# Both sequences of a pair in one low-rank product and one update

## The chip, the cores and the metric

The kernel runs on one core of a Trainium2 chip, all in float32. The metric is the device time of one execution in microseconds; of several executions the median is given. Beside it stands one execution that the hardware profiler recorded, with its own time and its span, from the first to the last instruction of the program.

## What is computed

Two layers with a residual each, on x of 8 sequences, 256 tokens, 1024 features:

```
# layer 0: one of several lora_A per sequence, rank 32
x = x + (x @ W0.T + (x @ lora_A0[i0[b]]) @ lora_B0.T * 0.5)
# layer 1: one of 32 adapters per sequence, rank 16, and a bias
x = x + (x @ W1.T + b + (x @ lora_A1[i1[b]]) @ lora_B1[i1[b]] * 2)
```

## The kernel before

**One matrix for both layers.** Both layers are linear, so the kernel multiplies them once: M = (W0 + 1)^T (W1 + 1)^T, of 1024 x 1024, and the output is x M plus an update of low rank for each sequence. This preparation takes the first 124 us of the span. After it come the 8 sequences in four pairs (the loop at L1164, `q` = 0 to 3).

**Seven products instead of eight, twice.** A pair's x has 256 tokens of each of two sequences, and 1024 features. It is cut into four blocks: `x["11"]` and `x["12"]` are the two halves of the features of the pair's first sequence, `x["21"]` and `x["22"]` those of the second. M is cut in four as well, and Winograd's form of Strassen's algorithm needs seven products of blocks, of sums of blocks (`Pair.sums_1` to `sums_4`) and of sums of M's blocks (`ops`). Each of the seven is done in the same way once more, on quarters: `product` (L517) runs seven steps of two matmuls each, 128x128 by 128x256, for which VectorE makes four sums of x's quarters (`z_sums`, L477) and `Operand.sums`, `sums_rest` those of M's (for the first pair these are made within the loop, under `early`). The fourth sum is an operand called `t4`.

**PSUM.** The eight banks are two sets of four, X and Y. A product fills the seven quarters of one set (`slot`, `BANK`); the next product goes to the other set. In Winograd's form some products add up on one another: with `first` False a product is accumulated on what its set holds. After a product the set is copied out by ScalarE (`keep`, L506) or added by VectorE to what was kept (`add_up`, L510: four additions, the bank of step 6 first and that of steps 3 and 4 last); `form` (L574) turns seven quarters into a block of 256 by 512, and `store` writes it out. In one turn of the loop, with P1 to P7 for its seven products:

| product | set | x operand | VectorE or ScalarE after it |
| --- | --- | --- | --- |
| P1 | X | x11 | keep(kept1) |
| P2 | Y | s1 | keep(kept5) |
| P3 | X, added to P1 | s2 | keep(kept2) |
| P4 | Y, added to P2 | s4 | add_up(kept2), form, store: first sequence, right half |
| P5 | X, added to P3 | s3 | add_up(kept5), form, store: second sequence, right half |
| P6 | Y, new | x12 | add_up(kept1), form, store: first sequence, left half |
| P7 | X, added to P5 | x22 | form from kept2 and X in the next turn: second sequence, left half |

In the table s1 to s4 stand for the sums in the code's order (`sq(0)` to `sq(3)`). X and Y change places from pair to pair.

**The low-rank part before.** For a sequence `b`, `down` (128 x 8 chunks x 64 columns) holds the down projections: 32 columns of layer 0 and 16 of layer 1 (the latter already multiplied with W0). `low_start` (L776) is one product with M = 64 output rows: TensorE's columns 0 to 63 take the first half of the features, columns 64 to 127 the second half at the same time, in 8 matmuls, and ScalarE scales the result and sets a row of ones for the bias (L788). The two partial sums must be added: `low_end` (L796) multiplies with the matrix `join`, which adds them, adds the cross term of the two layers, and writes the sum twice, into rows 0 to 63 and rows 64 to 127; ScalarE copies it back (L806). There is one such pair of calls for each sequence: for the pair's first sequence in P7 of the pair before (for the first pair in the last product of the preparation, the call of `chain.product` at L1136), for its second sequence in P1.

**The updates before.** `update` is low (256 tokens x 64 rows) times `up` (64 rows x 1024 columns: layer 0's up projection, layer 1's, and the bias). `add_update` (L536) adds it onto the accumulators of a product, in the slots 3, 2, 4 and 5: four matmuls that contract over 64 rows. They alternate between rows 0 to 63 and 64 to 127, which both hold the same sequence, so that two may run side by side in TensorE's rows. The stationary side is the low product of one half of the tokens, or the difference of both (`diff`, VectorE, L851); the moving side is a quarter of `up`'s columns, or for P7 the difference of `up`'s left and right half (`up21`, VectorE, L863). There is one update in P4 (first sequence, right half), P5 (second, right), P6 (first, left) and P7 (second, `up21`), after the product's third step.

**The order of the work** is written out by hand (`manual_schedule`): each engine's queue has the program's order, and semaphores are set between engines. TensorE, ScalarE, VectorE and GpSimd each run one queue; SP issues the loads, GpSimd most stores. In the preparation's last product ScalarE's queue has L788, L806, then the copy L1146; VectorE's queue has there `form(chain.keep5, X, ...)` at L1147, whose first instruction (L591) reads what L1146 copied, and behind it, in order, the sums for the first pair's M operands, `z_sums`, `pair.sums_2` (L841) and the first turn of the loop. `up` and `join` have two tiles each, one per sequence of a pair; `down` too.

Of the kernel before, what the change touches and what calls it, by code (L numbers as in the profile page):

```python
# [20 lines left out]
P = 128  # L21
# [3 lines left out]
MLOW = 64  # L25
ONES = 112
BIAS = 48
# [15 lines left out]
def kernel(  # L43
# [66 lines left out]

    joins = [const.tile([P, 2, MLOW], F32, tag=f"join{i}", name=f"join{i}") for i in range(NU)]
    cross = const.tile([P, B, R1], F32, tag="cross", name="cross")
    downs = [const.tile([P, NK, MLOW], F32, tag=f"down{i}", name=f"down{i}") for i in range(NV)]
    lows = a1.rearrange("p (n k) b r -> p n (k b r)", n=NLOW)
    diffs = [const.tile([P, P], F32, tag=f"diff{i}", name=f"diff{i}") for i in range(2)]
    s_all = const.tile([P, 2 * 4 * NB * P], F32, tag="s_all", name="s_all")
# [95 lines left out]

    def load_up(b: int):
        i = index(fixed1, b, N1)
        for copy in range(2):
            nc.sync.dma_start(
                ups[b % NU][copy * MLOW + R0 : copy * MLOW + RR, :],
                lora_b1[bass.ds(i, 1)].rearrange("o r d -> (o r) d"),
            )
# [294 lines left out]
    def low_region(ps):  # L514
        return ps[3][:, NQ:NH]

    def product(ps, x, z, op, first, update=None, low=None, plan=None, apart=None):  # L517

# [17 lines left out]
        def add_update():  # L536
            rows, diff, c0, c1 = update
            t0, t1 = rows[:, 0:P], rows[:, P:T]

            for n, (i, stat, mov) in enumerate(  # L540
                ((3, diff, c1), (2, t0, c0), (4, t1, c0), (5, t1, c1))
            ):
                half = slice(n % 2 * MLOW, (n % 2 + 1) * MLOW)
                into(i, stat[half], mov[half], False)

# [9 lines left out]
        if plan is None:  # L555
            plan = [1, 2, 4, add_update if update else None, 6, 5, 7, 3]
            if low:
                plan[5:5], plan[8:8] = low[:1], low[1:]
        for step in plan:
            if step == 0:  # L560
                add_update()
            elif callable(step):
                step()
            elif step is not None:
                a, b = operands[step]
                if step == 3 and apart is not None:
                    started.discard(BANK[3][0])
                for c in range(2):
                    into(step, a[:, c, :], f[b][:, c, :], c == 1, apart if step == 3 else None)

    def home(i: int):
        return work[:, i * NV7 * NQ : (i + 1) * NV7 * NQ]
# [202 lines left out]

    def low_start(b: int, x_b, pl):  # L776
        down = downs[b % NV]
        for k in range(NB):
            for half in range(2):
                nc.tensor.matmul(  # L780
                    pl[half * MLOW : (half + 1) * MLOW, :],
                    down[:, half * NB + k, :],
                    x_b[half][:, k, :],
                    start=(k == 0),
                    stop=(k == NB - 1),
                    skip_group_check=True,
                )
        nc.scalar.activation(  # L788
            lows[:, b % NLOW],
            pl,  # L790
            mybir.ActivationFunctionType.Identity,
            bias=shift[:, 0:1],
            scale=scale[:, 0:1],
        )

    def low_end(b: int, pl):  # L796
        low = lows[:, b % NLOW]
        nc.tensor.matmul(  # L798
            pl,
            joins[b % NU].rearrange("p u r -> p (u r)"),  # L800
            low,
            start=True,
            stop=True,
            skip_group_check=True,
        )
        nc.scalar.copy(low, pl)  # L806

    def fill_join(b: int):
        for half in range(2):
            rows = slice(half * MLOW, half * MLOW + R0)  # L810
            for copy in range(2):
                nc.gpsimd.tensor_scalar_mul(
                    joins[b % NU][rows, copy, R0:RR], cross[rows, b, :], L1_SCALING
                )

# [3 lines left out]
    class Pair:  # L819
# [4 lines left out]
        def __init__(self, q: int):  # L824
            self.q, self.b = q, (2 * q, 2 * q + 1)
            self.x = {}
            self.first, self.second = (sets[q % 2], sets[(q + 1) % 2])
            self.low = [lows[:, b % NLOW] for b in self.b]
            self.z = [z_homes[(NV7 * q + i - 1) % 3] for i in range(NV7)]
# [18 lines left out]

        def diff(self, n: int):
            low = self.low[n]  # L850
            nc.vector.tensor_tensor(diffs[n], low[:, 0:P], low[:, P:T], ALU.subtract)  # L851

        def update(self, n: int, h: int):
            cols = [ups[n][:, h * NH + i * NQ : h * NH + (i + 1) * NQ] for i in range(2)]
            return (self.low[n], diffs[n], *cols)

        def update21(self):

            return (self.low[1], diffs[1], up21[:, 0], up21[:, 1])

        def up21_sum(self):
            up = ups[1].rearrange("p (h i n) -> p h i n", h=2, i=2)
            nc.vector.tensor_tensor(up21, up[:, 0], up[:, 1], ALU.subtract)  # L863

    def end(pair, X, Y, v, w):
# [26 lines left out]
        def o22():  # L892
# [3 lines left out]
        plan = (  # L896
            0,
            lambda: nc.scalar.copy(v3, slot(X, 3)),
# [13 lines left out]
        )  # L912
        product(
            X, pair.xq("22"), pair.z[6], ops["t4"], False, pair.update21(), plan=plan, apart=p3
        )
        add(at(v, 3), p3, v3)
# [10 lines left out]
    with tc.manual_schedule(engines=ORDERED):  # L927
# [34 lines left out]
        nc.gpsimd.memset(shift, 0.0)  # L962
        nc.gpsimd.memset(shift[96:P], 1.0)
        nc.gpsimd.memset(shift[96:ONES], 0.0)
        nc.gpsimd.memset(fold, 0.0)
# [5 lines left out]
        for i in range(NV):  # L971
            nc.gpsimd.memset(downs[i], 0.0)
        for i in range(NU):
            nc.gpsimd.memset(joins[i], 0.0)
            for copy in range(2):
                sides = [ident[:, u * MLOW : u * MLOW + RR] for u in range(2)]
                nc.gpsimd.tensor_tensor(joins[i][:, copy, 0:RR], sides[0], sides[1], ALU.add)
                nc.gpsimd.tensor_copy(
                    joins[i][:, copy, BIAS : BIAS + 1], ident[:, ONES : ONES + 1]
                )  # L980

# [81 lines left out]
        for i in range(NU):  # L1063
            for copy in range(2):
                row = copy * MLOW + BIAS
                nc.sync.dma_start(ups[i][row : row + 1, :], bias1.rearrange("(o d) -> o d", o=1))
        for b in range(2):
            load_up(b)
        for i, which in enumerate(("21", "22")):
# [11 lines left out]
        for b in range(2):  # L1081
            fill_down(b)
            fill_join(b)
        one.product7()
# [38 lines left out]
        for which in ("21", "22"):  # L1123
# [17 lines left out]
            low=(  # L1141
                lambda: low_start(0, (pair.x["11"], pair.x["12"]), low_pl),
                lambda: low_end(0, low_pl),
# [15 lines left out]
        def load_down_later(b):  # L1159
            load_down(b)  # L1160
            fill_down(b)
            fill_join(b)

        for q in range(B // 2):  # L1164
            more = q + 1 < B // 2
            xs = pair.x
            early = q == 0
# [18 lines left out]
            if more:  # L1186
                load_next("11", "12", "21")
                load_down_later(after[0])
            kept1, kept5, kept2 = home(q % 2), home((q + 1) % 2), home(2)


            for task in pending:
                task()
            pl = low_region(Y)
            product(
                X,
                pair.xq("11"),
                pair.z[0],
                ops["11"],
                True,  # L1200
                low=(
                    lambda: low_start(b1_, (xs["21"], xs["22"]), pl),
                    lambda: low_end(b1_, pl),
                ),
            )
            keep(kept1, X)
            z_sums(pair.sq(1), pair.z[2])
            pair.diff(0)
            if early:
# [9 lines left out]
            if early:  # L1219
                ops["22"].sums_rest()  # L1220
                ops["21"].sums_dma()
            pair.diff(1)
            z_sums(pair.sq(3), pair.z[3])
# [15 lines left out]

            product(Y, pair.sq(3), pair.z[3], ops["22"], False, pair.update(0, 1))  # L1240
            if early:
# [6 lines left out]

            product(X, pair.sq(2), pair.z[4], ops["t3"], False, pair.update(1, 1))
            form(kept2)  # L1250
# [9 lines left out]

            product(Y, pair.xq("12"), pair.z[5], ops["21"], True, pair.update(0, 0))
            if more:
# [4 lines left out]
            if not more:  # L1267
# [12 lines left out]
                False,  # L1280
                pair.update21(),
                low=(
                    lambda: low_start(after[0], (following.x["11"], following.x["12"]), pl7),
                    lambda: low_end(after[0], pl7),
                ),
# [6 lines left out]
            following.sums_4()  # L1292
            for b in after:
                load_up(b)

# [47 lines left out]
```

## Time and profile before

| | us |
| --- | --- |
| median of 3 runs | 336.69 (335.87 to 337.17) |
| profiled execution | 336.44 |
| its span | 334.7 |
| TensorE busy | 329.2 |
| VectorE busy | 258.6 |
| ScalarE, GpSimd busy | 64.4, 65.3 |

The span is cut into 40 slices of 8.4 us, with a digit for the busy share of each engine in tenths. The granted clock of TensorE is 1.00 over the whole span. A line of the timeline gives the start, the length, the engine, the code's line, what is written and read, and the shape. `128*128 128x256` is a matmul with 128 rows and 128 columns of the array in use and a moving side of 256 columns; `64*128` uses half of the rows, `128*64` half of the columns. A matmul of the program makes two rows in float32. The length of a matmul is that of its way through the array; how close two follow is read from their starts. L526 is the line of `product`'s matmuls, L780 that of `low_start`, L798 that of `low_end`, L512 that of `add_up`, L486 that of `z_sums`, L436 that of `sums_rest`.

### The profile page before, as it was taken

What the parts mean: (1) busy time and instruction counts of PE and PEld (TensorE: products, weight loads), DVE (VectorE), ACT (ScalarE), POOL (GpSimd) and SP (SyncE); (2) the same over time, 40 slices, a digit from 0 to 9 for tenths busy, and PEclk for the clock granted to TensorE, in tenths of its full rate; (3) what the DMA queues carried; (4) which work ended last, traced back from release to release, by engine and by line L of the source; (5) the groups of instructions that cost most, each with busy time, mean ns of one, the idle gap of its engine ahead of it and who ended that gap; (6) DMA issues with size and microseconds to landing.
All of it is one profiled execution on the core that took longest, in us unless ns stands there. A gap on an engine that the chain in (4) does not pass through costs nothing.

```text
span 334.7 us, 4532 instructions
## 1 busy us (share of the span) xinstructions
PE 329.2 (98%) x1520; PEld 249.1 (74%) x1520; DVE 258.6 (77%) x498; ACT 64.4 (19%) x138; POOL 65.3 (20%) x121
## 2 busy tenths in 40 slices
PE   8999999999999999999999999999999999999996
PEld 8888434544488877888877887877888777788875
DVE  5886799569899999999997856985675986323964
ACT  1042224300034132440001330001330001322000
POOL 7003021540042232772023100012200010000000
DMA  7929992990062980686267400286400121100113
GB/s 213 208 94 192 227 241 58 161 178 21 2 94 66 197 132 14 110 135 105 95 179 210 85 0 0 77 217 158 111 8 0 65 94 63 66 0 1 65 63 125
DMA packets 66400, 34.53 MB, mean 103 GB/s; under 512 B 47301, under 2 KB 61125, under 8 KB 66377
## 3 DMA queue, kind: packets, MB, share of 16 engines
q1 hardware_dynamic: 56520, 21.13, 28.0%
q0 software_dynamic: 7680, 12.59, 17.6%
q10 hardware_dynamic: 2176, 0.52, 0.9%
q8 instruction: 12, 0.20, 0.2%
q14 instruction: 12, 0.09, 0.1%
HBM read 19.55 MB, written 8.39 MB: 83 GB/s over the span
## 4 chain that ended last, share of the span: by engine, by line
PE 87%; DMA 5%; DVE 3%; SPq 2%; ACTq 1%; issue 1%; ACT 0%; DVEq 0%
PE bank L526 66%; PE bank L285 10%; PE bank L780 4%; DMA units<-in_L_cond_W_dram 4%; PE bank L734 2%; DVE w1T L224 2%; PE bank L990 2%; SPq L170 2%; DMA work<-in_L_cond_lora_As_dram 1%; PE bank L798 1%; SPq L178 1%; ACTq L197 0%; DVE w1T L232 0%; ACTq L140 0%; PE bank L712 0%
## 5 line engine op out<-in xcount | busy, mean ns | idle before, releaser
L512 DVE TENSOR_TENSOR work<-bank,work 128x512 f32<-128x512 f32 (+1 forms) x56 | 32.7, 619 | 19.0 <-PE bank L526 18.8
L508 ACT COPY work<-bank 128x512 f32<-128x512 f32 (+1 forms) x60 | 27.6, 546 | 45.5 <-PE bank L526 45.0
L921 POOL DMA_DIRECT2D out_dram<-work x12 | 9.0, 754 | 101.4 <-DVE work L597 101.4
L526 PE MATMUL bank<-w0n,w1T 128*128 128x256 f32 x104 | 24.6, 384 | 0.0
L788 ACT ACTIVATE a<-bank,shift,scale 128x256 f32<-128x256 f32 x8 | 4.5, 564 | 103.3 <-PE bank L780 103.3
L224 DVE STREAM_TRANSPOSE w1T<-units 128x512 f32<-128x512 f32 (+1 forms) x20 | 17.5, 912 | 6.4 <-DMA units<-in_L_cond_W_dram 6.3
L526 PEld LDWEIGHTS bank<-w0n,w1T 128*128 128x128 f32 x104 | 19.3, 190 | 4.1 <-issue 1.7
L526 PE MATMUL bank<-w1T,s_all 128*128 128x256 f32 x88 | 22.3, 379 | 0.0
L526 PE MATMUL bank<-w0n,m 128*128 128x256 f32 x88 | 21.2, 384 | 0.0
L237 DVE STREAM_TRANSPOSE units<-units 128x512 f32<-128x512 f32 x32 | 19.9, 678 | 0.2
L526 PEld LDWEIGHTS bank<-w0n,m 128*128 128x128 f32 x88 | 16.4, 190 | 3.4 <-issue 1.4
L526 PEld LDWEIGHTS bank<-w1T,s_all 128*128 128x128 f32 x88 | 16.7, 190 | 2.3
L526 PE MATMUL bank<-tw,m 128*128 128x256 f32 x68 | 17.5, 382 | 0.0
L526 PE MATMUL bank<-tw,s_all 128*128 128x256 f32 x64 | 16.1, 379 | 0.0
L780 PE MATMUL bank<-units,down 128*64 128x256 f32 x128 | 15.6, 385 | 0.0
L526 PE MATMUL bank<-m,units 128*128 128x256 f32 x64 | 15.1, 379 | 0.0
L990 PE MATMUL bank<-w1T,w0n 128*128 128x256 f32 x64 | 14.5, 383 | 0.3 <-DVE w1T L232 0.3
L526 PEld LDWEIGHTS bank<-tw,m 128*128 128x128 f32 x68 | 12.8, 190 | 2.4 <-issue 0.7
L526 PE MATMUL bank<-w0n,s_all 128*128 128x256 f32 x56 | 14.4, 379 | 0.0
L285 PE MATMUL bank<-tw,s_all 128*128 128x512 f32 x32 | 14.3, 595 | 0.0
L734 PE MATMUL bank<-w0n,a 128*128 128x512 f32 x32 | 14.3, 599 | 0.0
L285 PE MATMUL bank<-w1T,s_all 128*128 128x512 f32 x32 | 14.1, 592 | 0.0
(255 smaller groups left out, 658.7 us busy)
## 6 DMA issues: line engine op xcount, KB each, us to landing
units<-in_x_dram SPq DMA_DIRECT2D x128, 64.0 KB, 2.4
out_dram<-work POOLq DMA_DIRECT2D x12, 512.0 KB, 3.4
w0n<-in_L_cond_W_dram SPq DMA_DIRECT2D x16, 256.0 KB, 6.4
units<-in_L_cond_W_dram SPq DMA_DIRECT2D x12, 256.0 KB, 6.7
out_dram<-work SPq DMA_DIRECT2D x3, 512.0 KB, 2.8
units<-in_L_cond_W_dram SPq DMA_DIRECT2D x8, 128.0 KB, 4.3
down<-in_L_cond_lora_A_dram SPq DMA_DIRECT2D x32, 32.0 KB, 2.9
up<-in_L_cond_lora_Bs_dram SPq DMA_DIRECT2D x16, 64.0 KB, 3.0
```

The source lines that it names most:

```text
L170: nc.sync.dma_start(wq[g * SQ : (g + 1) * SQ, lo:hi, :], w1[rows, cols].rearrange("(t q) c -> q t c", q=SQ),)
L224: nc.vector.transpose(w1T[:, k, cols].rearrange("p (t q) -> p t q", q=SQ), wq[:, lo:hi].rearrange("p t (q m) -> p m t q", m=NB)[:, k % NB],)
L237: nc.vector.transpose(xT[:, NX * j : NX * (j + 1), :].rearrange("p c (t q) -> p c t q", q=SQ), xq[:, :, j, :].rearrange("p t (q c) -> p c ...
L285: nc.tensor.matmul(pm, a[:, k, :], b(k), start=first and k == 0, stop=(k == NB - 1), skip_group_check=not first,)
L508: nc.scalar.copy(at_home(v, n), whole(ps, n))
L512: nc.vector.tensor_tensor(at_home(v, n), whole(ps, n), at_home(v, n), ALU.add)
L526: nc.tensor.matmul(slot(ps, i) if dst is None else dst, lhs, rhs, start=BANK[i][0] not in started, stop=stop, skip_group_check=True,)
L734: nc.tensor.matmul(pm, a1[:, k].rearrange("p b r -> p (b r)"), w0n[:, k, h * NH : (h + 1) * NH], start=(k == 0), stop=(k == NK - 1),)
L780: nc.tensor.matmul(pl[half * MLOW : (half + 1) * MLOW, :], down[:, half * NB + k, :], x_b[half][:, k, :], start=(k == 0), stop=(k == NB - ...
L788: nc.scalar.activation(lows[:, b % NLOW], pl, mybir.ActivationFunctionType.Identity, bias=shift[:, 0:1], scale=scale[:, 0:1],)
L921: eng.dma_start(out[b, :, h * NH : (h + 1) * NH].rearrange("(j p) d -> p j d", p=P), ob[:, 0:D].rearrange("p (j d) -> p j d", d=NH),)
L990: nc.tensor.matmul(g.p1[:, cols], g.a[0][:, k, :], w1T[:, k, cols], start=False, stop=(k == NB - 1), skip_group_check=True,)
```

## The change

The columns 0 to 63 of a low-rank product now belong to the pair's first sequence, the columns 64 to 127 to its second, each over all features: 16 matmuls in one call for the pair, in P7 of the pair before (for the first pair in the preparation's last product). There is no second call in P1. No partial sums are left; `join` is one matrix of 128 x 128 that adds the cross term within each half, one `low_end` per pair. `up` holds one sequence in each half, and each `diff` is of the whole pair.

An update now does both sequences: for each of the slots 3, 2, 4 and 5 one matmul from rows 0 to 63 and one from rows 64 to 127, into two different sets. P4 takes the right halves: the first sequence's into Y, P4's own set, the second's into X, onto which P5 will be added. P6 takes the left halves: the first sequence's into Y, its own set, and the second's `up21` into X, onto which P7 will be added. P5 and P7 have none. The place in the product moves from behind step 4 (the third) to behind five of the seven steps in P4 and behind six in P6 (`late`).

```diff
-    joins = [const.tile([P, 2, MLOW], F32, tag=f"join{i}", name=f"join{i}") for i in range(NU)]
+    join = const.tile([P, P], F32, tag="join", name="join")
-    diffs = [const.tile([P, P], F32, tag=f"diff{i}", name=f"diff{i}") for i in range(2)]
+    diff = const.tile([P, P], F32, tag="diff", name="diff")
...
-    def load_up(b: int):
-        i = index(fixed1, b, N1)
-        for copy in range(2):
+    def load_up(q: int):
+        for n in range(2):
+            i = index(fixed1, 2 * q + n, N1)
             nc.sync.dma_start(
-                ups[b % NU][copy * MLOW + R0 : copy * MLOW + RR, :],
+                ups[q % NU][n * MLOW + R0 : n * MLOW + RR, :],
...
         def add_update():
-            rows, diff, c0, c1 = update
+            rows, both = update
             t0, t1 = rows[:, 0:P], rows[:, P:T]
-            for n, (i, stat, mov) in enumerate(
-                ((3, diff, c1), (2, t0, c0), (4, t1, c0), (5, t1, c1))
-            ):
-                half = slice(n % 2 * MLOW, (n % 2 + 1) * MLOW)
-                into(i, stat[half], mov[half], False)
+            for i, stat, c in ((3, diff, 1), (2, t0, 0), (4, t1, 0), (5, t1, 1)):
+                for n, (to, cols) in enumerate(both):
+                    half = slice(n * MLOW, (n + 1) * MLOW)
+                    if to is ps:
+                        into(i, stat[half], cols[c][half], False)
+                    else:
+                        nc.tensor.matmul(
+                            slot(to, i),
+                            stat[half],
+                            cols[c][half],
+                            start=False,
+                            stop=False,
+                            skip_group_check=True,
+                        )
...
-            plan = [1, 2, 4, add_update if update else None, 6, 5, 7, 3]
+            plan = [1, 2, 4, 6, 5, 7, 3]
+            if update:
+                plan.insert(late, add_update)
             if low:
-                plan[5:5], plan[8:8] = low[:1], low[1:]
+                plan[4:4], plan[7:7] = low[:1], low[1:]
...
-    def low_start(b: int, x_b, pl):
-        down = downs[b % NV]
-        for k in range(NB):
-            for half in range(2):
+    def low_start(q: int, x_b, pl):
+        for k in range(NK):
+            for n in range(2):
                 nc.tensor.matmul(
-                    pl[half * MLOW : (half + 1) * MLOW, :],
-                    down[:, half * NB + k, :],
-                    x_b[half][:, k, :],
+                    pl[n * MLOW : (n + 1) * MLOW, :],
+                    downs[n][:, k, :],
+                    x_b[f"{n + 1}{k // NB + 1}"][:, k % NB, :],
...
-    def fill_join(b: int):
-        for half in range(2):
-            rows = slice(half * MLOW, half * MLOW + R0)
-            for copy in range(2):
-                nc.gpsimd.tensor_scalar_mul(
-                    joins[b % NU][rows, copy, R0:RR], cross[rows, b, :], L1_SCALING
-                )
+    def fill_join(q: int):
+        for n in range(2):
+            rows, first = slice(n * MLOW, n * MLOW + R0), n * MLOW
+            nc.gpsimd.tensor_scalar_mul(
+                join[rows, first + R0 : first + RR], cross[rows, 2 * q + n, :], L1_SCALING
+            )
...
+        def update(self, h: int):
+            first = [self.up[:, h * NH + i * NQ : h * NH + (i + 1) * NQ] for i in range(2)]
+            second = first if h else [up21[:, 0], up21[:, 1]]
+            return self.low, ((self.second, first), (self.first, second))
...
-            product(
-                X,
-                pair.xq("11"),
-                pair.z[0],
-                ops["11"],
-                True,
-                low=(
-                    lambda: low_start(b1_, (xs["21"], xs["22"]), pl),
-                    lambda: low_end(b1_, pl),
-                ),
-            )
+            product(X, pair.xq("11"), pair.z[0], ops["11"], True)
...
-            pair.diff(0)
+            pair.diff()
...
-            pair.diff(1)
...
-            product(Y, pair.sq(3), pair.z[3], ops["22"], False, pair.update(0, 1))
+            product(Y, pair.sq(3), pair.z[3], ops["22"], False, pair.update(1))
...
-            product(X, pair.sq(2), pair.z[4], ops["t3"], False, pair.update(1, 1))
+            product(X, pair.sq(2), pair.z[4], ops["t3"], False)
...
-            product(Y, pair.xq("12"), pair.z[5], ops["21"], True, pair.update(0, 0))
+            product(Y, pair.xq("12"), pair.z[5], ops["21"], True, pair.update(0), late=6)
...
-            for b in after:
-                load_up(b)
+            load_up(q + 1)
```

In the set-up on GpSimd the shift has two memsets more and `join` three instructions where the two joins had ten. P7 (`product` with `ops["t4"]`, and `end` in the last turn) has no update any more.

## The prediction

> **What bounds the kernel now.** I read the page first: the engines' totals, the slices, the chain that ended last.
>
> ```profile
> span 334.7 us, 4532 instructions
> PE 329.2 (98%) x1520; PEld 249.1 (74%) x1520; DVE 258.6 (77%) x498; ACT 64.4 (19%) x138; POOL 65.3 (20%) x121
> PE   8999999999999999999999999999999999999996
> DVE  5886799569899999999997856985675986323964
> PE 87%; DMA 5%; DVE 3%; SPq 2%; ACTq 1%; issue 1%; ACT 0%; DVEq 0%
> ```
>
> TensorE works in every slice and is 87% of the chain, so a matmul less is time less. VectorE is as full only in slices 12 to 21. Second, the list of TensorE's waits, whole:
>
> ```profile
> PE bank L950 <- POOL ident masks.py:199: 1.4, 1, 1.4
> PE bank L526 <- DVE bank L632: 0.4, 1, 0.4
> PE bank L990 <- DVE w1T L232: 0.3, 1, 0.3
> ```
>
> All three lie before 28 us. From 61 us on TensorE waits for nobody, but that says nothing of how close the others are behind it. So third, VectorE's waits between 124.3 and 182.1 us, again the whole list:
>
> ```profile
> DVE work L591 <- ACT work L1146: 0.6, 1, 0.6
> ```
>
> In those 58 us VectorE waits once and then runs without a pause: if that one wait grows, all behind it moves.
>
> **Prices.** One update and one low-rank product, from TensorE's timeline (start, length, shape, rows; a program matmul is two rows):
>
> ```profile
> 146.80 1.03 PE L526 MATMUL bank<-w1T,s_all 128*128 128x256 f32 x4
> 147.75 0.48 PE L526 MATMUL bank<-up,diff 64*128 64x256 f32 x1
> 147.76 0.48 PE L526 MATMUL bank<-up,a 64*128 64x256 f32 x1
> 148.07 0.38 PE L526 MATMUL bank<-up,diff 64*128 64x256 f32 x1
> 148.08 0.81 PE L526 MATMUL bank<-up,a 64*128 64x256 f32 x5
> 148.82 1.99 PE L526 MATMUL bank<-w1T 128*128 128x256 f32 x8
> 150.65 1.03 PE L526 MATMUL bank<-w1T,m 128*128 128x256 f32 x4
> ```
>
> ```profile
> 118.47 1.03 PE L526 MATMUL bank<-w0n,m 128*128 128x256 f32 x4
> 119.43 1.95 PE L780 MATMUL bank<-units,down 128*64 128x256 f32 x16
> 121.31 1.99 PE L526 MATMUL bank<-w0n,m 128*128 128x256 f32 x8
> 123.14 0.59 PE L798 MATMUL bank<-a,join 128*128 128x256 f32 x2
> 123.57 1.03 PE L526 MATMUL bank<-tw,m 128*128 128x256 f32 x4
> ```
>
> Plain rows start 0.216 apart, so a product of 14 matmuls takes 6.05.
> - Update of 4 matmuls: due at 146.80 + 4 x 0.216 = 147.66; the 8 plain rows after it end at 150.65. 2.99 - 8 x 0.216 = **1.26**. Its 8 rows run two at a time (147.75 and 147.76): 4 x 0.216 = 0.86. The other 0.40 is the change of shape, in and out.
> - Low-rank product of 8 matmuls: due at 119.33, followed by 8 plain rows up to 123.14: 3.81 - 1.73 = **2.08**: 16 rows in twos 1.73, change of shape 0.35.
> - join: 123.57 - 123.14 = **0.43**.
>
> **The change on TensorE, per pair.** The matmuls of update (16) and low-rank product (16) stay as many. They come in two updates of 8 (2 x (1.73 + 0.40) = 4.26) in place of four of 4 (5.04), in one low product of 16 (3.45 + 0.35 = 3.80) in place of two of 8 (4.16), and one join goes (0.43). 10.06 becomes 8.49: 1.57 less, **6.3 us** in four pairs. This holds if the two row halves still run in twos when one writes one set of four banks and the other the other set. The trace shows twos into different banks of one set only: 0.216 a pair if so, 0.43 if not; I take 0.216, the nearest row, since both halves and the alternation stay.
>
> The change of shape itself: measured 0.40 and 0.35. The Trainium skill (TensorEngine Tiling, Key Properties) says that a change of tiling mode drains TensorE; TensorE: Matmul & The Clock Gate, Single matmul latency, puts a drain at about 175 ns. Two drains a block, 12 blocks fewer, would by an estimate from that page give 4.2 us where the rows give 8 x 0.40 + 4 x 0.35 = 4.6: the time would be 0.4 longer.
>
> **Off TensorE.** Four ACTIVATE (0.56) and four copies (0.37) of ScalarE go, hidden now by 45 to 103 us of its waits. GpSimd's join fills go from 8 to 2 a pair; at 137 to 143 us they end over 30 us before their matmul. Of its set-up on the joins most goes and two memsets come; it ends at 9.2 and GpSimd then waits to 25. SP issues 2 loads of up a pair less (four took 2.8) into a tile that nobody reads any more, so it stops there no longer. All nothing, in both directions. One diff (0.28 long, 0.20 to the next start) leaves VectorE at 141.86.
>
> **What is late next.** Call P0 the chain's last product and P1 to P7 those of the first pair. In P0 the low product now does both sequences: +1.73. VectorE's one wait hangs on it:
>
> ```profile
> 124.45 0.42 DVE L591 TENSOR_TENSOR work<-bank,work 128x256 f32<-128x256 f32 x1 [0.58 <-ACT work L1146]
> 135.97 1.22 DVE L841 TENSOR_TENSOR s_all<-s_all,units 128x1024 f32<-128x1024 f32 x1
> 159.97 0.69 DVE L436 TENSOR_TENSOR w0n<-m,w0n 128x512 f32<-128x512 f32 x1
> 163.24 2.21 DVE L512 TENSOR_TENSOR work<-bank,work 128x256 f32<-128x256 f32 x4
> ```
>
> L591 reads what ScalarE copies at L1146, behind its copy of the low product, behind join. So all VectorE work from 124.45 is 1.73 later, and 1.53 from 142 (the diff gone), while TensorE, with no low product in P1, comes earlier. Old times in brackets:
> - P0 ends 126.16 (124.43), P1 132.2 (132.98), P2 138.26 (139.03). P2's nearest need, its second z sum, has 0.2 left.
> - P3's first operand is L841: 137.19 + 1.73 = 138.9. TensorE waits 0.7 and 0.1 to restart; ends 145.1 (145.07).
> - P4 with 8 updates ends 153.3 (152.38). Its X half also waits for ScalarE's copies of P3, about 147.1, and is due at 149.4. P5 ends 159.3 (159.68).
> - P6's third operand, t4 by L436: 160.66 + 1.53 = 162.2, due at 161.0: 1.2 of waiting.
> - P6's update writes X too, so it must wait for the four additions L512: 165.45 + 1.53 = 167.0. Due at 162.2 + 8 x 0.43 = 165.7: 1.3 of waiting. Behind it in order stand the rest of the update, operand 3 and P7. P6 ends 170.0 (166.99), P7 with the long low product 180.3 (176.80), the next P1 186.3 (185.34).
>
> So 1.0 is lost at that point where 2.36 should be gained: the waits cost **3.3 us**. In the later pairs VectorE idles (3.1 us at 182); its additions before P6 end at 212.94, 0.9 after P5's end, and the update there is due 5.2 after it: no wait. Half of the second pair's x loads free their place in P7, now some 3 us later; the last landed at 189.5 as VectorE turned them, so VectorE is late there too, but it idles 1.6 us at 195.9, and P7 needs them only then. Three pairs of updates (0.78 each) and two low products (0.79) are still to gain: 3.9. At the end VectorE's last adds just fit behind the shorter P7: 0 to 0.2, counted in the rounding.
>
> Sum: 334.7 + 1.0 - 3.9 = 331.8, and the 1.74 that lie around the span (336.44 - 334.7): **333.5 us**. The profiled execution, 336.44, is 0.25 under the median shown, 336.69.
>
> Such waits could do more than last. TensorE stood still before restarting at 15.70 and 27.27, at a granted clock of 1.00 in the profile. The Trainium skill (TensorE: Matmul & The Clock Gate, Why this matters for your kernels) warns of idle gaps above some 3 us, which slow the clock. By that rule waits of 0.7 to 1.3 cost their length and nothing else; only 3.3 in one piece would add to it. No run here shows that.
>
> **Rivals.**
> - *VectorE is not that late.* For it: the page's rows put P2's need 0.2 from the edge, so small shifts decide; some waits may overlap. Then up to the whole 6.3 comes: 336.44 - 6.3 = 330.1. Against it: VectorE's list has no gap in which to catch up. 0.13.
> - *The new wait on X also bites in later pairs, or VectorE slips further in the first.* Three more waits of up to 1 us: 336.0 to 336.5, no change. Against it: 4 us of slack in the second pair. 0.11.
> - *The halves don't run side by side* once they write two sets of banks or one of them waits: 8 blocks, each 8 x 0.216 = 1.73 longer: 13.8 more, 347, slower. It decides from three such blocks in eight (5.2 us, past no change). For it: no row shows such a pair. Against it: the same halves in twos at 147.75, into different banks. 0.07.
>
> **How the numbers follow.** Forecast 0.67, rivals 0.13, 0.11, 0.07, the rest 0.02 slower. Range 330.9 to 336.0: from most of the first rival up to the second. Faster by over 0.5% (about what a measurement of this kernel can tell) means under 334.8: nearly the whole forecast and the first rival, 0.80; same 0.11; slower 0.09.
>
> **What will show it.** 6.3 less of TensorE's work: updates with 16 rows in about 1.9, starts in pairs; low blocks of 32 rows in 3.6; four joins. New waits of TensorE for L841, L436 and L512's successors, near 139, 161 and 166 us, and none later. Wrong would be: updates of 3.6 us; TensorE still without waits; waits in pairs two to four; or VectorE's form not moved by 1.73.

## The result, and the profile after

The changed kernel takes 334.13 us (median of 20 runs, 332.81 to 336.18), the kernel before 336.84 (20 runs) in the same series. The ratio taken over all runs is 0.9915, with a 95% interval of 0.9901 to 0.9930 (that of the two medians is 0.9920). Forecast were 333.5 and a range of 330.9 to 336.0. The profiled execution took 333.67 with a span of 331.9, where the forecast had 331.8.

The changed kernel's page, with the lines that answer to those shown of the kernel before:

```profile
span 331.9 us, 4436 instructions
PE 324.2 (98%) x1512; PEld 249.7 (75%) x1512; DVE 258.5 (78%) x494; ACT 60.6 (18%) x130; POOL 53.5 (16%) x92
PE   8999999999999999999899999999999999999996
PE 84%; DVE 8%; SPq 3%; DMA 3%; issue 1%; ACT 1%; ACTq 0%; DVEq 0%
```

TensorE is 5.0 us less busy, but the span is only 2.8 shorter. (It is not 6.3 less: of the 3.3 us that the stops of TensorE cost, worked out below, the profile counts 2.1 as idle and the rest as busy.) Where the rest went shows in two places: VectorE's share of the chain went from 3% to 8%, and one slice of TensorE, the 20th, which begins at 157.6 us, fell from 9 to 8. The list of TensorE's waits has three entries that the kernel before did not have (engine and line, who ended the wait, us in total, times, longest):

```profile
PE bank L527 <- DVE w0n L436: 1.0, 1, 1.0
...
PE bank L527 <- DVE s_all L842: 0.7, 1, 0.7
...
PE bank L547 <- DVE work L512: 0.5, 1, 0.5
```

L527 and L547 are the matmuls of `product` and of an update onto the other set, L842 is `pair.sums_2`. VectorE's waits between 124 and 182 us:

```profile
DVE work L601 <- ACT work L1139: 2.3, 1, 2.3
DVE work L601 <- ACT work L1266: 0.9, 1, 0.9
```

L601 is the first instruction of `form`, which was L591 before. The wait that was 0.6 is 2.3. (The second, behind P7, waits for TensorE.) What hangs on it, in VectorE's timeline of the changed kernel:

```profile
126.34 0.42 DVE L601 TENSOR_TENSOR work<-bank,work 128x256 f32<-128x256 f32 x1 [2.32 <-ACT work L1139]
...
137.86 1.22 DVE L842 TENSOR_TENSOR s_all<-s_all,units 128x1024 f32<-128x1024 f32 x1
...
161.69 0.69 DVE L436 TENSOR_TENSOR w0n<-m,w0n 128x512 f32<-128x512 f32 x1
...
164.96 2.21 DVE L512 TENSOR_TENSOR work<-bank,work 128x256 f32<-128x256 f32 x4
```

Against the kernel before they start 1.89, 1.89, 1.72 and 1.72 later. P0 itself began 0.17 later in this execution (116.05, not 115.88), so the change's part is 1.72, and 1.55 after the second diff is gone. P6 of the first pair, in TensorE's timeline:

```profile
159.56 1.89 PE L527 MATMUL bank<-m,units 128*128 128x256 f32 x8
162.43 1.13 PE L527 MATMUL bank<-w0n,units 128*128 128x256 f32 x4 [0.98 <-DVE w0n L436]
163.40 2.75 PE L527 MATMUL bank<-w0n,w1T 128*128 128x256 f32 x12
166.08 0.70 PE L527 MATMUL bank<-up,diff 64*128 64x256 f32 x2
167.23 0.48 PE L547 MATMUL bank<-w1T,diff 64*128 64x256 f32 x1 [0.45 <-DVE work L512]
167.23 0.48 PE L527 MATMUL bank<-up,a 64*128 64x256 f32 x1
...
169.15 1.13 PE L527 MATMUL bank<-m,w1T 128*128 128x256 f32 x4
```

TensorE stops three times. The first stop lies ahead of this view, in P3: the last four rows of P2 start from 137.55, so P3 was due at 137.55 + 4 x 0.216 = 138.41, and it started at 139.23. The second is in the second line: P6's third operand starts at 162.43, just as L436 ends. The third is in the update. Its first two rows go into Y; then everything stands until the additions on X are done (164.96 + 2.21 = 167.17), and the next row of the half that could go on (the second line at 167.23) stands with it. Where nothing is waited for, in the second pair, a whole update of 16 rows looks like this:

```profile
201.11 1.89 PE L527 MATMUL bank<-w1T,m 128*128 128x256 f32 x8
202.93 0.48 PE L527 MATMUL bank<-up,diff 64*128 64x256 f32 x1
202.94 0.48 PE L547 MATMUL bank<-up,diff 64*128 64x256 f32 x1
...
204.86 1.13 PE L527 MATMUL bank<-w1T,m 128*128 128x256 f32 x4
205.83 1.03 PE L527 MATMUL bank<-m,m 128*128 128x256 f32 x4
```

Rows in twos, 7 ns apart, into two sets. Due at 201.11 + 8 x 0.216 = 202.84; 205.83 - 202.84 - 4 x 0.216 = 2.13, to the hundredth the forecast's price. The low-rank block, in P0:

```profile
118.64 1.03 PE L527 MATMUL bank<-w0n,m 128*128 128x256 f32 x4
119.60 3.67 PE L789 MATMUL bank<-units,down 128*64 128x256 f32 x32
123.20 1.99 PE L527 MATMUL bank<-w0n,m 128*128 128x256 f32 x8
125.03 0.59 PE L807 MATMUL bank<-a,join 128*128 128x256 f32 x2
```

Due at 119.50, 5.53 to the join, less 1.73: 3.80, as forecast.

Two stretches are good measures, since they don't hold the preparation, whose length differs by up to 2 us between profiled executions. **The stretch of a pair**, from one P7's low block to the next: 52.36 before (8.55 to the low block in P1 and 43.81 on to the next P7), 50.79 after, 1.57 less. **The first pair's stretch**, from P0's start to the low block of the first pair's P7: 55.91 before, 57.61 after, 1.70 more. The tail behind the last matmul row's start is 3.52 and 3.61.

### The profile page after: what moved, and what is told of

Its sections match the earlier page's. It is cut to its first block, busy times and chain, and to the rows that moved or that the text cites. A ratio compares the mean times of both kernels' runs of the same rounds, so it can differ in the third digit from the quotient of the medians.

```text
span 331.9 us, 4436 instructions
## 1 busy us (share of the span) xinstructions
PE 324.2 (98%) x1512; PEld 249.7 (75%) x1512; DVE 258.5 (78%) x494; ACT 60.6 (18%) x130; POOL 53.5 (16%) x92
## 4 chain that ended last, share of the span: by engine, by line
PE 84%; DVE 8%; SPq 3%; DMA 3%; issue 1%; ACT 1%; ACTq 0%; DVEq 0%
PE bank L527 59%; PE bank L285 10%; PE bank L789 4%; PE bank L744 4%; DMA units<-in_L_cond_W_dram 2%; PE bank L984 2%; PE bank L722 1%; DVE work L512 1%; SPq L154 1%; DVE units L237 1%; SPq L169 1%; DMA down<-in_L_cond_lora_A_dram 1%; DVE w1T L224 1%; PE bank L547 1%; DVE w1T L486 1%
## 5 line engine op out<-in xcount | busy, mean ns | idle before, releaser
L527 PE MATMUL bank<-w0n,w1T 128*128 128x256 f32 x104 | 24.1, 379 | 0.0
L527 PE MATMUL bank<-w1T,s_all 128*128 128x256 f32 x88 | 22.3, 380 | 0.7 <-DVE s_all L842 0.7
L237 DVE STREAM_TRANSPOSE units<-units 128x512 f32<-128x512 f32 x32 | 20.1, 683 | 2.5 <-DMA units<-in_x_dram 2.4
L527 PEld LDWEIGHTS bank<-w0n,w1T 128*128 128x128 f32 x104 | 19.8, 190 | 2.7
L527 PE MATMUL bank<-w0n,m 128*128 128x256 f32 x88 | 20.9, 380 | 0.0
L527 PEld LDWEIGHTS bank<-w1T,s_all 128*128 128x128 f32 x88 | 16.6, 190 | 3.2 <-issue 1.0
L797 ACT ACTIVATE a<-bank,shift,scale 128x256 f32<-128x256 f32 x4 | 2.3, 564 | 89.5 <-PE bank L789 83.7
L527 PEld LDWEIGHTS bank<-w0n,m 128*128 128x128 f32 x88 | 16.6, 190 | 2.6 <-issue 0.4
L527 PE MATMUL bank<-tw,m 128*128 128x256 f32 x68 | 17.4, 381 | 0.0
L527 PE MATMUL bank<-tw,s_all 128*128 128x256 f32 x64 | 16.1, 379 | 0.0
L527 PE MATMUL bank<-m,units 128*128 128x256 f32 x64 | 15.1, 379 | 0.0
L789 PE MATMUL bank<-units,down 128*64 128x256 f32 x128 | 14.7, 382 | 0.0
L527 PEld LDWEIGHTS bank<-tw,m 128*128 128x128 f32 x68 | 12.8, 190 | 2.1 <-issue 0.4
L527 PE MATMUL bank<-w0n,s_all 128*128 128x256 f32 x56 | 14.4, 379 | 0.0
L984 PEld LDWEIGHTS bank<-w1T,w0n 128*128 128x128 f32 x64 | 12.3, 196 | 2.4 <-DVE w1T L232 1.3
```

The source lines that it names most:

```text
L237: nc.vector.transpose(xT[:, NX * j : NX * (j + 1), :].rearrange("p c (t q) -> p c t q", q=SQ), xq[:, :, j, :].rearrange("p t (q c) -> p c ...
L527: nc.tensor.matmul(slot(ps, i) if dst is None else dst, lhs, rhs, start=BANK[i][0] not in started, stop=stop, skip_group_check=True,)
L789: nc.tensor.matmul(pl[n * MLOW : (n + 1) * MLOW, :], downs[n][:, k, :], x_b[f"{n + 1}{k // NB + 1}"][:, k % NB, :], start=(k == 0), stop=( ...
L984: nc.tensor.matmul(g.p1[:, cols], g.a[0][:, k, :], w1T[:, k, cols], start=False, stop=(k == NB - 1), skip_group_check=True,)
```

## The experiments

Two theories stood. **One debt**: TensorE's three waits in the first pair all come from one place, VectorE's `form` that a longer P0 makes late; the debt is paid at the latest where P6's update needs X's additions, and only that point sets the time. **Rival**: the waits come from the new updates themselves (two sets, a restart, more to wait for), each with its own price. The ratios, taken over all runs as above, are to the kernel before on the same chip. The stretches are from the one profiled execution of each run.

**r0: the changed kernel again**, as a measure for r1 to r3.

> The changed kernel as it is, on the chip of the next three runs, as their measure. Both theories: 334.1 us, 0.9915 of the kernel before (0.990 to 0.993 so far), with TensorE's three waits in the first pair at 139, 162 and 167 us: 0.65, 0.98 and 0.45 us of idle time.

Measured: 333.43 us, 0.9898 (0.9874 to 0.9921). Idle times 0.65, 0.96 and 0.45; the first pair's stretch 57.58. It repeats.

**r2: t4 earlier.**

```diff
+            if early:
+                ops["21"].sums_rest()
             form(kept2)
             store(kept2, b0_, 1)
-            if early:
-                ops["21"].sums_rest()
```

> In the first pair VectorE makes the operand t4 for P6 before the form of the first sequence's right half and not after it: ready at 159.9 and not at 162.4, so that TensorE's wait of 0.98 (1.14 with the restart) in P6 goes. X's additions end where they ended, at 167.2. Theory (one debt): the wait for X in P6 grows by what the wait for t4 lost, to some 2 us, P7 starts at 170.1 as before, and the time stays at 334.1. Rival (each wait has its own price): 1.1 less, 333.0.

Measured: 334.23 us, 0.9931 (0.9906 to 0.9955). In r2's timeline of TensorE P6's third operand follows without a pause, and the wait for X is longer by about as much:

```profile
159.09 1.89 PE L527 MATMUL bank<-m,units 128*128 128x256 f32 x8
160.82 1.03 PE L527 MATMUL bank<-w0n,units 128*128 128x256 f32 x4
161.68 2.75 PE L527 MATMUL bank<-w0n,w1T 128*128 128x256 f32 x12
164.37 0.70 PE L527 MATMUL bank<-up,diff 64*128 64x256 f32 x2
166.75 0.48 PE L547 MATMUL bank<-w1T,diff 64*128 64x256 f32 x1 [1.69 <-DVE work L512]
```

The first pair's stretch is 57.59, against 57.58. A wait of 1 us was taken away and nothing was gained, to 10 ns: the debt is one, and it moved on to the next place where it falls due. The times can't tell r2 from r0, the intervals overlap; the stretch can.

**r3: the update behind the last step.**

```diff
-            product(Y, pair.xq("12"), pair.z[5], ops["21"], True, pair.update(0), late=6)
+            product(Y, pair.xq("12"), pair.z[5], ops["21"], True, pair.update(0), late=7)
```

> P6's update stands behind all seven steps and not behind six, in every pair. Theory: in the first pair the last step (0.86 us) is done while TensorE would wait for X's additions, so P7 starts 0.8 to 0.9 earlier; in the other pairs nothing changes, since nothing is waited for there: 333.3. Rival (the wait is not for X's additions but for the row halves' change of shape or for up21): it moves along with the update, no gain.

Measured: 333.50 us, 0.9897 (0.9871 to 0.9923). The first pair's stretch is 56.73, 0.85 less than in r0: a step's work now stands where TensorE waited, as the theory said, and the wait for X, the last one, is gone from the list; those for L842 and t4 are still there. But in the last pair the additions on Y come later behind P6, and the tail grew from 3.60 to 3.99. That leaves 0.46, which the times don't show against r0. That the tail would grow was not expected.

**r1: the low block behind P0.** Here the debt itself is taken away: P0's 14 matmuls end first, and ScalarE's copy needs nothing more. The low block follows on TensorE right behind them, while ScalarE copies and before VectorE's `form` begins.

```diff
-        chain.product(
-            X,
-            "22",
-            "t4",
-            False,
-            low=(
-                lambda: low_start(0, pair.x, low_pl),
-                lambda: low_end(0, low_pl),
-            ),
-        )
+        chain.product(X, "22", "t4", False)
         nc.scalar.copy(chain.keep5[:, SLOT[1] * NQ : (SLOT[1] + 1) * NQ], slot(X, 1))
+        low_start(0, pair.x, low_pl)
...
-            product(X, pair.xq("11"), pair.z[0], ops["11"], True)
+            first_low = [1, 2, 4, lambda: low_end(0, low_region(Y)), 6, 5, 7, 3]
+            product(
+                X, pair.xq("11"), pair.z[0], ops["11"], True, plan=first_low if early else None
+            )
```

> The same work, but the first low-rank product stands behind the last product of the preparation (P0) and not within it, and its join in P1. So P0 ends at 122.1 us and not at 126.3, and VectorE's form can begin when VectorE is free, at 124.0, and not at 126.34. Theory (the waits are one debt: VectorE's late start, paid where P6's update needs X's additions): all VectorE work up to P6 is 2.3 earlier, the waits for the sum s2 and for t4 go, X's additions end at 164.9 and not at 167.2, and P7 starts 2.3 earlier: span 329.6, time 331.8, 0.985 of the kernel before. Rival (the waits come from the new updates themselves, the restart of TensorE on two sets of banks): the wait in P6 stays at some 0.5 to 1 us wherever VectorE stands, and the time goes down by less than 1.

Measured: 342.47 us, 1.0171 (1.0145 to 1.0197), far from both. The experiment was at fault. `join` is one matrix now, and GpSimd's fill for the second pair stands ahead of P1 in the program: by that order this join uses the second pair's cross term (so r1 computes something else in the first pair), and it had to wait until GpSimd, behind with its DMAs, had filled it. From r1's list of waits, and its stretches before, in, just behind and further behind the wait (us, PE busy, PEld, DVE, ACT, POOL, the granted clock, the DMA share, GB/s):

```profile
PE bank L807 <- POOL join L813: 9.1, 1, 9.1
```

```profile
121.00:128.60 7.60, 7.58 (x50) 5.11 (x48) 7.29 (x15) 2.12 (x4) 0.89 (x1) 1.00 0.44 70
128.60:137.70 9.10, 0.02 (x1) 0.02 (x1) 8.93 (x15) 0.00 (x0) 4.76 (x7) 0.65 0.50 72
137.70:141.60 3.90, 3.90 (x9) 3.14 (x10) 2.83 (x5) 0.37 (x1) 0.30 (x1) 0.50 0.24 34
141.60:150.00 8.40, 8.40 (x40) 7.35 (x39) 6.54 (x12) 1.99 (x5) 0.00 (x0) 1.00 0.00 0
```

VectorE's form did begin at 123.87, as expected; the rest tells nothing of the theories. It does tell two other things: the place of a fill decides as soon as two tiles have become one, and in a stop of 9.1 us TensorE's clock fell to half (see the end).

**r4: the same, with the fill behind P1's join.** To r1's edit:

```diff
                 load_down_later(after[0])
-                fill_join(q + 1)
...
+            if more:
+                fill_join(q + 1)
             keep(kept1, X)
```

> As r1, but GpSimd fills the next pair's join only after P1's join matmul was issued, so that it reads its own pair's and waits for no fill. Theory (one debt): VectorE's form begins at 123.9 and not at 126.34; the waits for s2 and t4 go; X's additions end 2.47 earlier, and TensorE waits for them 0.6 still, since it too comes earlier; from P0's start to the low block of P7 55.1 us and not 57.6; time 2.5 less than the changed kernel: 331.0 to 331.6, 0.983 of the kernel before. Rival (waits from the updates themselves): 0.5 less at most.

Measured: 331.75 us, 0.9849 (0.9824 to 0.9875). The first pair's stretch is 55.20 (expected 55.1). Of the three waits one is left, and TensorE's timeline shows what it costs:

```profile
PE bank L547 <- DVE work L512: 0.2, 1, 0.2
```

```profile
164.83 0.70 PE L527 MATMUL bank<-up,diff 64*128 64x256 f32 x2
...
167.62 1.13 PE L527 MATMUL bank<-m,w1T 128*128 128x256 f32 x4
```

2.4 us of the lost 3.3 came back, with the same matmuls on TensorE and with the same updates. So it is VectorE's late start that made TensorE wait, and not the updates by themselves. The rest is in this update: it takes 2.79 from its first row to the plain row behind it, and 1.93 where nothing is waited for (202.93 to 204.86 above). That is 0.86, of which the list of waits counts only 0.2.

**r5: and X's additions first.** To r4:

```diff
+            pair.up21_sum()
+            add_up(kept5, X)
             z_sums(pair.xq("22"), pair.z[6])
             if early:
                 ops["t4"].sums_rest()
-            pair.up21_sum()
-            add_up(kept5, X)
```

> As r4, and in every pair VectorE makes up21 and P5's additions ahead of the sums for P7. In the first pair X's additions end some 2 us earlier, so that the last wait, 0.6 for X, goes as well, and what is left of the gain on TensorE comes: from P0's start to the low block of P7 54.3 to 54.5 us, 0.6 less than r4, 330.4 to 331.0. If the debt then falls on the sums for P7, TensorE waits at P7 and r4's time stays.

Measured: 330.40 us, 0.9812 (0.9787 to 0.9837), the fastest of all, though its interval overlaps with r4's. The stretch is 54.34, 0.86 less than r4's and 1.57 less than before the change: the whole gain of a pair. The update in P6 now runs in twos from its first row:

```profile
165.32 0.48 PE L527 MATMUL bank<-up,diff 64*128 64x256 f32 x1
165.33 0.48 PE L547 MATMUL bank<-w1T,diff 64*128 64x256 f32 x1
...
167.25 1.13 PE L527 MATMUL bank<-m,w1T 128*128 128x256 f32 x4
```

**r6: each update in two.** This measures the other half of the sum, the change of shape.

```diff
-        def add_update():
+        def add_update(part=slice(0, 4)):
...
-            for i, stat, c in ((3, diff, 1), (2, t0, 0), (4, t1, 0), (5, t1, 1)):
+            for i, stat, c in ((3, diff, 1), (2, t0, 0), (4, t1, 0), (5, t1, 1))[part]:
...
-                plan.insert(late, add_update)
+                plan.insert(late + 1, lambda: add_update(slice(2, 4)))
+                plan.insert(late, lambda: add_update(slice(0, 2)))
```

> The changed kernel with each update cut in two: the slots 3 and 2 where it stood, 4 and 5 one step of the product later. The same matmuls, one more change of shape per update. Theory (0.40 for each change of shape, in and out, is where half of the gain came from): from the low block of one P7 to the next 51.6 us and not 50.79, the time 2.4 to 2.8 longer: 336.2 to 336.9, as slow as the kernel before. Rival (the gain is only the joins and the overlap of more rows): 50.8, no change.

Measured: 337.15 us, 1.0012 (0.9995 to 1.0028): the whole gain is gone. The pair's stretch is 51.58, 0.79 more for two cuts: 0.40 each. (A small part of the lost time is elsewhere: the tail is 4.00 and not 3.61.) An update in r6's second pair:

```profile
202.83 0.48 PE L527 MATMUL bank<-up,diff 64*128 64x256 f32 x1
...
203.90 1.13 PE L527 MATMUL bank<-w1T,m 128*128 128x256 f32 x4
204.96 0.48 PE L527 MATMUL bank<-up,a 64*128 64x256 f32 x1
...
206.02 1.13 PE L527 MATMUL bank<-m,m 128*128 128x256 f32 x4
```

From 202.83 to 203.90 pass 1.07 for 4 x 0.216 = 0.86, and from there to 204.96 1.06 for the 0.86 of four plain rows: each stretch of a shape takes some 0.20 more, 0.40 for a block of another shape, in and out. Half of it can be seen in the lengths: each first piece in a new shape (0.48, 1.13) is 0.10 longer than one that follows its like (0.38, 1.03).

**r7: the halves in turn.**

```diff
-            for i, stat, c in ((3, diff, 1), (2, t0, 0), (4, t1, 0), (5, t1, 1)):
-                for n, (to, cols) in enumerate(both):
+            for n, (to, cols) in enumerate(both):
+                for i, stat, c in ((3, diff, 1), (2, t0, 0), (4, t1, 0), (5, t1, 1)):
```

> The changed kernel, with the four matmuls of an update's first half before the four of its second, and not in turn. Theory (TensorE takes its matmuls in order, so two halves run side by side only where they alternate): each update 1.73 longer, from P7 to P7 54.2 us and not 50.79; the first pair 1.2 longer, where the waits hide the rest; 345 us, slower than before. Rival (each half of the rows has a queue of its own, so the order does not matter): 50.8 and no change.

Measured: 339.22 us, 1.0078 (1.0049 to 1.0108); the pair's stretch 52.72, 1.93 more, 0.97 for each update and not 1.73. Neither theory. r7's timeline shows how far the halves overlap:

```profile
202.22 0.70 PE L527 MATMUL bank<-up,diff 64*128 64x256 f32 x2
202.76 0.81 PE L527 MATMUL bank<-up,a 64*128 64x256 f32 x3
203.19 0.48 PE L547 MATMUL bank<-up,diff 64*128 64x256 f32 x1
203.40 0.38 PE L527 MATMUL bank<-up,a 64*128 64x256 f32 x1
203.51 0.38 PE L547 MATMUL bank<-up,diff 64*128 64x256 f32 x1
203.62 0.38 PE L527 MATMUL bank<-up,a 64*128 64x256 f32 x1
203.73 0.38 PE L547 MATMUL bank<-up,a 64*128 64x256 f32 x1
203.84 0.38 PE L527 MATMUL bank<-up,a 64*128 64x256 f32 x1
203.94 1.24 PE L547 MATMUL bank<-up,a 64*128 64x256 f32 x5
```

L527 is the first half with 8 rows, L547 the second. The second half's first row starts with the fifth of the first half, and its last five run alone. In the first pair the stretch is 57.59, no longer than in the changed kernel: there the longer update in P4 used up time in which P6 would have waited for t4, and the one in P6 is no longer than the changed kernel's with its wait (3.07 us both times, from the first row to the plain row behind it). The expectation of 1.2 more had not seen this.

**r8: the kernel before, with the low-rank products moved alone.**

```diff
             low=(
-                lambda: low_start(0, (pair.x["11"], pair.x["12"]), low_pl),
-                lambda: low_end(0, low_pl),
+                lambda: [
+                    low_start(0, (pair.x["11"], pair.x["12"]), low_pl),
+                    low_start(1, (pair.x["21"], pair.x["22"]), low_region(X)),
+                ],
+                lambda: [low_end(0, low_pl), low_end(1, low_region(X))],
             ),
...
-                low=(
+                low=None
+                if early
+                else (
                     lambda: low_start(b1_, (xs["21"], xs["22"]), pl),
                     lambda: low_end(b1_, pl),
                 ),
```

> The kernel before, with one part of the change alone: the low-rank products of both sequences of the first pair stand in P0, as two products with two joins as before; the updates as before. Theory (a longer P0 makes VectorE late, and TensorE pays for it later): P0 2.16 longer, VectorE's form 2.16 later; TensorE waits 0.7 for s2 at P3 and 1.0 for t4 in P6, where the kernel before waits for nothing; from P0's start to the low block of P7 57.4 us and not 55.9; 1.5 more than the kernel before, 338.3, 1.0045. Rival (only the new update on X makes TensorE wait): no waits, one change of shape less, 0.3 less than before.

Measured: 338.81 us, 1.0050 (1.0031 to 1.0070); the first pair's stretch 57.48 (expected 57.4, before 55.91). VectorE's form waits 2.75 us (P0 is 2.15 longer here, where the change made it 1.73 longer), and TensorE has the first two waits of the changed kernel without any of its updates:

```profile
PE bank L526 <- DVE w0n L436: 0.8, 1, 0.8
PE bank L526 <- DVE s_all L841: 0.6, 1, 0.6
```

So the low product's place alone makes the debt. The kernel before had been early enough, and not by much: t4 was ready at 160.66 there, and P6 used it at 161.41.

**r9: the kernel before, with r5's order alone** (the edits of r4 and r5, with the joins' fills of the first sequence behind P1).

> The kernel before with r5's order alone: the first low product behind P0, its join in P1, and in every pair up21 and P5's additions ahead of the sums for P7. Theory (r5's order pays back the debt that the change made, and the kernel before has none): no gain, 55.9 us from P0's start to P7's low block, 1.000 of the kernel before. Rival (the order is a gain of its own): 1 to 3 us less.

Measured: 336.47 us, 0.9999 (0.9982 to 1.0016), the first pair's stretch 55.91 as before. r5's order is worth nothing where there is no debt.

## Why the prediction was right

Forecast 333.5, measured 334.13; the span 331.8 and 331.9. By its steps:

- *Prices on TensorE.* Update 2.13, low block 3.80, 1.57 less per pair: 2.13, 3.80 and 1.57 measured. r6 measured the 0.40 for a change of shape by itself, r7 that the halves run side by side only as long as they alternate closely. Of the 6.3 us, 12 changes of shape are 4.6 by these prices and four joins 1.7; that no partial sums are left to be joined is the smaller part. No run took the joins alone; their 0.43 is read from the rows. Of the two rates for a drain that the prediction weighed, the rows' 0.40 held for the updates and not the estimate of 0.35 that it worked out from the Trainium skill's figure (TensorE: Matmul & The Clock Gate, Single matmul latency, which gives 175 ns for a bf16 matmul, beside the time of its moving columns); r6 has 0.79 for two. For a low block the rows' own price is 0.35 as well.
- *VectorE later by 1.73, then 1.53.* Measured 1.72 and 1.55.
- *The waits.* For L842 0.7 to 0.8 forecast; its start was put off by 0.82 (from 138.41 to 139.23). For t4 1.2; 1.14. For X 1.3; the update takes 3.07 from its first row to the plain row behind it (166.08 to 169.15), and 1.93 where nothing is waited for: 1.14. (Only 0.83 of it lies between two starts, since two rows of the Y half go ahead of the wait, and the X half has to run its last rows alone.) With some 0.1 more behind each of the first two stops that is 3.3, as forecast. The first pair's stretch says the same: it is 1.70 longer where it should have been 1.57 shorter, 3.27 in all.
- *No wait in later pairs.* None: 50.79 in each of them. VectorE did wait 2.4 us for x's loads (transposes L237 for the transfers of x), of which the prediction had said that it would have room for it, and it had.
- *The tail.* 0 to 0.2 forecast, 0.09 measured.
- *Rivals.* VectorE less late: no, but r4 and r5 show what it would have given, 330.4 (the rival's figure was 330.1). Halves not side by side: no in the changed kernel; r7 made it so in part, and its price was half of what the prediction had put.

Of the 0.6 between 333.5 and 334.13, 0.4 comes from where the forecast started: it counted from an execution of 336.44, and the kernel before has a median of 336.84 here. The saving was forecast as 2.9 and is 2.7 between the medians. The rest is not explained step by step, and that the spans agree to 0.1 is in part luck: the preparation's length differs by more from one execution to the next (P0 began between 115.4 and 117.4 us in the profiles here).

So why less than half of the 6.3 us arrived is settled: r8 makes the debt without the updates, r4 and r5 pay it back with the updates, r2 shows that it is one, r9 that it did not exist before.

## What to carry to other kernels

An engine that waits for nobody in the profile may still get another engine's results with less than a microsecond to spare (0.75 for t4 here): before moving work ahead on the busy engine, list what the other engine starts right behind it, and follow that queue to the next place where its slack is spent. Several waits in a row that come from one late start are one debt. Taking away one ahead of the last gave nothing (r2), and work put into the last gave only that work's length (r3, 0.85); the cheap cure is the order at the start (here: let the product end ahead of the low-rank block, so that its copy waits for nothing). Small matmuls in another shape of the array are better in few long blocks, with the two halves alternating one by one.

## What was not expected of the hardware

- With the halves in turn, TensorE overlapped them only in part: in r7 the second half began with the first half's fifth row of eight, that is with its third matmul of four, and not with the first or after the last. 0.97 us were lost in each update by the order alone. It looks as if TensorE sees only a few matmuls ahead; no run here shows what sets the distance.
- The two rows of one float32 matmul need not follow each other: in the kernel before and in the changed one the first row of the second half starts some 7 ns after the first row of the first half, and 0.3 us ahead of the first half's second row (147.754, 147.761 and 148.074 before).
- Stops of up to 2.1 us between two starts (r2) left the granted clock at 1.00. The stop of 9.1 us in r1 did not: the granted clock is 1.00 up to 131.2 us and 0.50 from 131.4, some 2.8 us after TensorE's last row had ended at 128.58. It stayed there for the rest of the stop and for the 3.9 us behind it, in which rows started 0.427 apart in place of 0.216. The Trainium skill (TensorE: Matmul & The Clock Gate, Why this matters for your kernels) warns of idle gaps above some 3 us. r1 and r2 lie on its two sides and agree with it; r1's one stop is all that shows where the clock went down.
